# Moving q and k to other byte places in SBUF, in a convolution-attention kernel bound by TensorE

## Chip, cores, metric

One core of a Trainium2 chip. The metric is the device time of one execution in microseconds (us). Each program ran three times or more. Durations of single matmuls are in nanoseconds (ns). In the lines of the profile, PE is TensorE, PEld its weight loads, DVE VectorE, ACT ScalarE and POOL GpSimd; L324 is line 324 of that run's kernel.

## The reference, cut

```python
# x: (4, 64, 64, 256) float32
q = einsum('bwhc,cd->bwhd', x, Wq) + bq          # d = 128
k = einsum('bwhc,cd->bwhd', x, Wk) + bk
v = einsum('bwhc,cd->bwhd', x, Wv) + bv          # d = 256
pq, pk, pv = (t.reshape(B, -1, 4096) for t in (q, k, v))   # a plain reshape, no transpose
attention = softmax(einsum('bcn,bcm->bnm', pq, pk), axis=-1)
out = einsum('bcm,bnm->bcn', pv, attention)
return gamma * out.reshape(B, W, H, C) + x
```

## The kernel before: the parts that matter

float32 products are made from float32r matmuls. q, k, v and the weights x of the softmax are each split: h is the high part, l = x - h the low part, d a difference that carries the rest. A step makes 12 energy matmuls (sa twice and sb once, for four tiles of 128 keys) and 24 for the output: 8 of h with vh, 8 of l with vl (both add into the accumulators a) and 8 of d with vd (into bb). A group is 8 steps for 256 queries; there are 512 steps in all. TensorE's order in the steady loop is always energies, vh, vl, vd, energies.

```python
xpool, xtpool, qkv = pool("xpool", 3), pool("xtpool", 3), pool("qkv", 1)
pool("pad", 1).tile([P, 16], F32, name="pad")
ppool = pool("ppool", 2)                       # x, y, h, l, d
pool("pad2", 1).tile([P, 16], F32, name="pad2")
work, kpool = pool("work", 2), pool("kpool", 3)
...
vh = qkv.tile([P, NM, VC], F32R, tag="vh", name="vh")      # VC = 260: 256 channels, two columns of ones
vl = qkv.tile([P, NM, VC], F32R, tag="vl", name="vl")
vd = qkv.tile([P, NM, C], F32R, tag="vd", name="vd")       # C = 256
...
def energy(b, u, k):
    ...
    for i in range(2):
        for to, f, first, last in ((sa, 0, True, False), (sa, 1, False, True), (sb, 2, True, True)):
            nc.tensor.matmul(to[:, i], kt[:, 2 * k + i, f, :], q[:, f], start=first, stop=last)
...
def attend(b, u):
    ...
    for left, right in ((h, vh), (l, vl), (d, vd)):
        for j in range(NJ):
            out_ = bb[:, j, :] if left is d else acc[j]
            for i in range(4):
                m = 2 * t + i // 2 + NI * (i % 2)
                nc.tensor.matmul(out_, left[:, i, j * P : (j + 1) * P], right[:, m, : out_.shape[1]], ...)
```

In each matmul the first tile (k, h, l, d) is the stationary operand, loaded as weights: 128 columns, 512 bytes of a partition (LDWEIGHTS 128x128 in the profile). The second (q, vh, vl, vd) is the moving one: 256 columns, 1024 bytes, or 258 for vh and vl (MATMUL 128x256 and 128x258), whose two columns of ones give the softmax sums.

**Place** below means a tile's first byte in its partition modulo 256, read from the built program (the prediction gives the same modulo 512). vd is at 32 and d at 96. Rows of vh and vl are 1040 bytes apart, so their places walk in steps of 16. Before, q is at 160 and k at 224.

## Time and profile before

| | |
|---|---|
| time before, median | 2494.4 us (2494.1 to 2496.5 in 3 runs) |
| TensorE busy | 99% of the span |
| energies, 6144 matmuls | 747.4 us from start to start |
| h with vh, 4096 | 494.9 us |
| l with vl, 4096 | 489.8 us |
| d with vd, 4096 | 475.4 us |
| all other matmuls | 276.2 us |

The last five rows are sums of **spacings**. A spacing is the time from a matmul's start to the start of the next one on TensorE. The records of matmuls that follow each other overlap (those of h with vh are 284 ns long in the mean, and start 121 ns apart), so their lengths do not add up to the time; the spacings do. Throughout, a spacing of 114 ns or less is called fast, 117 to 119 slow, and over 140 a gap.

### The profile page before, as it was taken

Reading aid. Unit: us, or ns where it says so; the run is one execution under the profiler, and the core shown is the slowest. Engines: PE = TensorE matmul, PEld = TensorE weight load, DVE = VectorE, ACT = ScalarE, POOL = GpSimd, SP = SyncE. Lnnn points to the kernel's source line nnn. Section 1 sums busy time; section 2 is a strip of 40 time slices with the busy share of each in tenths; the row PEclk is TensorE's granted clock in tenths of the full one; section 3 lists DMA queues with packets and bytes.
Section 4 is the critical chain, followed back from the end, with each engine's and each line's share of the span. In section 5 each row is a group of like instructions: output and inputs, shape, how many; then the busy total and the mean of one; then the engine's idle time right before and its main releaser. Section 6 shows DMA issues by size and latency. Waiting matters only on the chain.

```text
span 2494.6 us, 50085 instructions
## 1 busy us (share of the span) xinstructions
PE 2481.1 (99%) x19982; PEld 2438.4 (98%) x19982; DVE 2106.9 (84%) x2440; ACT 1809.1 (73%) x3138; POOL 425.7 (17%) x780
## 2 busy tenths in 40 slices
PE   9999999999999999999999999999999999999998
PEld 8999999999899999999989999999998999999998
DVE  5888888888698888888869888888886988888887
ACT  5777777777677777777667777777766777777775
POOL 4211111111411111111041111111114111111110
PEclk9999999999999999999999999999999999999999
DMA  7666666664766666666477666666648666666663
GB/s 231 222 195 210 201 201 200 198 202 156 235 220 193 206 199 203 206 188 208 139 244 223 197 193 209 201 208 195 191 145 253 217 201 196 203 203 207 199 193 110
DMA packets 137408, 498.92 MB, mean 200 GB/s; under 512 B 15536, under 2 KB 57264, under 8 KB 137168
## 3 DMA queue, kind: packets, MB, share of 16 engines
q0 software_dynamic: 92320, 453.17, 58.0%
q1 hardware_dynamic: 44304, 42.22, 5.7%
q8 instruction: 160, 2.62, 0.4%
q14 instruction: 80, 0.66, 0.1%
q10 hardware_dynamic: 544, 0.26, 0.0%
HBM read 445.25 MB, written 50.33 MB: 199 GB/s over the span
## 4 chain that ended last, share of the span: by engine, by line
PE 95%; ACT 2%; DVE 1%; issue 1%; DMA 1%; POOL 0%; SPq 0%; ACTq 0%; DVEq 0%; POOLq 0%
PE a L370 38%; PE sa L320 19%; PE bb L370 18%; PE sb L320 10%; PE qk L136 4%; PE v L157 4%; PE ot L416 1%; PE xt L123 1%; ACT h L339 1%; DVE x L334 1%; ACT x L324 0%; ACT y L324 0%; ACT vh L284 0%; DMA kf<-f 0%; DVE vd L287 0%
## 5 line engine op out<-in xcount | busy, mean ns | idle before, releaser
L324 ACT ACTIVATE x<-sa 128x512 f32<-128x512 f32 x1024 | 609.4, 595 | 398.3 <-PE sa L320 330.0
L320 PE MATMUL sa<-q,k 128*128 128x256 f32 x4096 | 757.4, 283 | 1.4 <-ACT x L324 0.9
L334 DVE TENSOR_TENSOR x<-x,y 128x1024 f32<-128x1024 f32 x512 | 625.9, 1222 | 155.6 <-ACT y L324 155.6
L320 PEld LDWEIGHTS sa<-q,k 128*128 128x128 f32 x4096 | 625.7, 189 | 2.8 <-ACT x L324 1.7
L345 DVE TENSOR_TENSOR l<-x,h 128x1024 fp32r<-128x1024 f32 x512 | 624.6, 1220 | 0.0
L348 DVE SCALAR_TENSOR_TENSOR d<-h,x 128x1024 fp32r<-128x1024 f32 x512 | 624.5, 1220 | 0.0
L324 ACT ACTIVATE y<-sb 128x512 f32<-128x512 f32 x1024 | 613.2, 599 | 0.0
L320 PE MATMUL sb<-q,k 128*128 128x256 f32 x2048 | 582.0, 284 | 0.0
L370 PE MATMUL a<-vh,h 128*128 128x258 f32 x4096 | 578.3, 284 | 0.0
L339 ACT ACTIVATE h<-x 128x1024 fp32r<-128x1024 f32 x512 | 543.7, 1062 | 43.1 <-DVE x L334 38.3
L370 PE MATMUL a<-vl,l 128*128 128x258 f32 x4096 | 573.3, 282 | 0.0
L370 PE MATMUL bb<-vd,d 128*128 128x256 f32 x4096 | 557.3, 278 | 0.0
L304 POOL DMA_DIRECT2D k<-kf x512 | 280.5, 548 | 1485.6 <-PE sb L320 1467.0
L370 PEld LDWEIGHTS a<-vh,h 128*128 128x128 f32 x4096 | 526.3, 190 | 0.0
L370 PEld LDWEIGHTS a<-vl,l 128*128 128x128 f32 x4096 | 526.2, 190 | 0.0
L370 PEld LDWEIGHTS bb<-vd,d 128*128 128x128 f32 x4096 | 514.1, 188 | 0.0
L320 PEld LDWEIGHTS sb<-q,k 128*128 128x128 f32 x2048 | 384.5, 188 | 9.4 <-ACT y L324 1.4
L136 PE MATMUL qk<-wqk_sb,xts 128*128 128x256 f32 x512 | 122.8, 383 | 0.0
L400 DVE SCALAR_TENSOR_TENSOR o<-a,o 128x256 f32<-128x256 f32 x126 | 47.6, 420 | 86.9 <-ACT o L380 86.9
L157 PE MATMUL v<-xts,wv_sb 128*128 128x256 f32 x512 | 120.3, 379 | 0.0
L157 PEld LDWEIGHTS v<-xts,wv_sb 128*128 128x128 f32 x512 | 97.3, 190 | 13.2
L408 ACT ACTIVATE o<-o,r 128x256 f32<-128x256 f32 x126 | 57.6, 505 | 72.4 <-DVE r L391 72.4
(54 smaller groups left out, 931.0 us busy)
## 6 DMA issues: line engine op xcount, KB each, us to landing
k<-kf POOLq DMA_DIRECT2D x512, 768.0 KB, 4.8
x<-in_x_dram SPq DMA_DIRECT2D x128, 256.0 KB, 3.6
kf<-f POOLq DMA_DIRECT2D x64, 384.0 KB, 3.8
out_dram<-x POOLq DMA_DIRECT2D x63, 256.0 KB, 2.5
qd<-qks POOLq DMA_DIRECT2D x128, 64.0 KB, 3.0
qr<-qd SPq DMA_DIRECT2D x64, 128.0 KB, 3.0
wv_sb<-in_L_conv_Wv_dram POOLq DMA_DIRECT2D x1, 256.0 KB, 5.7
out_dram<-x SPq DMA_DIRECT2D x1, 256.0 KB, 4.1
```

What stands on the lines that cost most here:

```text
L136: nc.tensor.matmul(qk[:, s, :], self.xt[i][:, k, s, :], wqk_sb[:, k, :], start=(k == 0), stop=(k == KC - 1),)
L157: nc.tensor.matmul(vp[:, eh, :], wv_sb[:, k, eh * P : (eh + 1) * P], self.xt[i][:, k].rearrange("p s a -> p (s a)"), start=(k == 0), stop= ...
L304: nc.gpsimd.dma_start(t.rearrange("p (i s) f d -> p i s (f d)", s=2), kf[b, u % NU])
L320: nc.tensor.matmul(to[:, i], kt[:, 2 * k + i, f, :], q[:, f], start=first, stop=last)
L324: nc.scalar.activation(to[:, 2 * k : 2 * k + 2, :], sp.rearrange("p i j d -> p i (j d)"), AF.Exp, scale=scale,)
L334: nc.vector.tensor_tensor(x, x, y, ALU.mult)
L339: nc.scalar.activation(h, units[b, u], AF.Identity, scale=UPPER)
L345: nc.vector.tensor_tensor(l, x, h.bitcast(F32), ALU.subtract)
L348: nc.vector.scalar_tensor_tensor(d, h.bitcast(F32), 1.0 + E, x, ALU.mult, ALU.subtract)
L370: nc.tensor.matmul(out_, left[:, i, j * P : (j + 1) * P], right[:, m, : out_.shape[1]], start=(t == i == 0 and (left is h or left is d and ...
L400: nc.vector.scalar_tensor_tensor(o[:, j, :], a[:, :C], 1.0 + E, o[:, j, :], ALU.mult, ALU.add)
L408: nc.scalar.activation(o[:, j, :], o[:, j, :], AF.Identity, scale=r[:, j : j + 1])
```

## The change

The intent is to give the energies the same operand places as the vd matmuls that run just before them. Raw q, the loaded q before it is split, drops to one buffer, which makes the room. q's first buffer goes to vd's place, k to d's, and q's second buffer 256 bytes on from the first one's place modulo 512.

```diff
-        pool("pad2", 1).tile([P, 16], F32, name="pad2")
-        work, kpool = pool("work", 2), pool("kpool", 3)
+        pool("pad2", 1).tile([P, 112], F32, name="pad2")
+        work = pool("work", 2)
+        pool("pad3", 1).tile([P, 64], F32, name="pad3")
+        kpool = pool("kpool", 3)
...
-            t = work.tile([P, NJ, P], F32, tag="qr", name=f"qr_{b}_{g}")
+            t = work.tile([P, NJ, P], F32, tag="qr", name=f"qr_{b}_{g}", bufs=1)
...
-            t = work.tile([P, 3, NJ, P], F32R, tag="q", name=f"q_{b}_{g}")
+            t = work.tile([P, 6 * P + 64 * (g % 2)], F32R, tag=f"q{g % 2}", name=f"q_{b}_{g}", bufs=1)
+            t = t[:, 64 * (g % 2) :].rearrange("p (f j d) -> p f j d", f=3, j=NJ)
```

## The prediction

> **What bounds the kernel now.** I read the page's engine shares first, then the chain that ended last, then the groups of instructions, then the engine's waits, then a timeline of TensorE alone.
>
> ```profile
> PE 2481.1 (99%) x19982; PEld 2438.4 (98%) x19982; DVE 2106.9 (84%) x2440; ACT 1809.1 (73%) x3138; POOL 425.7 (17%) x780
> ...
> PE 95%; ACT 2%; DVE 1%; issue 1%; DMA 1%; POOL 0%; SPq 0%; ACTq 0%; DVEq 0%; POOLq 0%
> ```
>
> TensorE and its weight loads are busy all the time and carry 95% of the chain; VectorE has 16% to spare, ScalarE 27%. TensorE's recorded waits for others sum to about 7 us of 2494. So only two things can move the time: the number of matmuls, or the time from one matmul to the next. The instruction order shows the same instructions in the same order on every engine, so the number stays.
>
> ```profile
> L320 PE MATMUL sa<-q,k 128*128 128x256 f32 x4096 | 757.4, 283 | 1.4 <-ACT x L324 0.9 <-DVE q L261 0.5
> L320 PE MATMUL sb<-q,k 128*128 128x256 f32 x2048 | 582.0, 284 | 0.0
> L370 PE MATMUL a<-vh,h 128*128 128x258 f32 x4096 | 578.3, 284 | 0.0
> L370 PE MATMUL a<-vl,l 128*128 128x258 f32 x4096 | 573.3, 282 | 0.0
> L370 PE MATMUL bb<-vd,d 128*128 128x256 f32 x4096 | 557.3, 278 | 0.0
> ```
>
> The second number after the bar is the mean length of one record. The records overlap, so it isn't the spacing, but the differences are real: vd,d is a matmul of the same 256 columns as sa and sb and is 5 to 6 ns shorter. The timeline gives spacing: take the difference of two groups' starts and divide by the count.
>
> ```profile
> 365.14 1.08 PE L370 MATMUL bb<-vd,d 128*128 128x256 f32 x8
> 366.06 0.40 PE L320 MATMUL sa<-q,k 128*128 128x256 f32 x2
> 366.29 0.28 PE L320 MATMUL sb<-q,k 128*128 128x256 f32 x1
> 366.41 0.40 PE L320 MATMUL sa<-q,k 128*128 128x256 f32 x2
> 366.65 0.28 PE L320 MATMUL sb<-q,k 128*128 128x256 f32 x1
> 366.76 0.40 PE L320 MATMUL sa<-q,k 128*128 128x256 f32 x2
> 367.00 0.28 PE L320 MATMUL sb<-q,k 128*128 128x256 f32 x1
> 367.12 0.40 PE L320 MATMUL sa<-q,k 128*128 128x256 f32 x2
> 367.35 0.28 PE L320 MATMUL sb<-q,k 128*128 128x256 f32 x1
> 367.48 1.11 PE L370 MATMUL a<-vh,h 128*128 128x258 f32 x8
> ```
>
> vd,d: 366.06 - 365.14 = 0.92 us for 8, 115 ns each. Energies: 367.48 - 366.06 = 1.42 us for 12, 118 ns each.
>
> **What single starts show.** I joined the start of each of the 19982 matmuls with its operands' addresses in the built program (the order agrees one to one). Spacing here is from one start to the next. Three findings carry the prediction.
>
> - Spacings fall into classes, not a continuum. In vd,d the fourth to seventh matmul of a run of eight is at 113 or 114 ns in 340 to 450 of 512 runs; a run starts at 120.5 ns (mean) and falls by 118.1, 116.0, 114.5 to 114.0. The energies sit at 117 to 119 ns: 4601 of 6144 at 117 to 119, only 562 at 113 or 114; leaving out 227 that are over 140 ns, the mean is 117.6.
> - Both classes hold themselves. After a 113 or 114 in an energy run the next one is that again in 90% of cases; after 117 to 119 again 117 to 119 in 89%. In vd,d the fast class is kept at 96%, but the slow one only at 45%.
> - The energies enter from vd,d, which ends at 113 or 114 in 374 of the 436 cases where energies follow at once. The first energy matmul is then never fast (0 of 374).
>
> At that entry the addresses change. v's d form lies at byte 288 modulo 512 and d at 352; q lies at 416 and k at 480, in all their buffers. The differences are the same (64), the positions are not. In the changed program q's first buffer is at 288, its second at 32, all of k at 352.
>
> [...]equal matmuls differ by 4 to 5 ns, in classes that go with the operands. [...]this trace never has a steady run below 113, so I take 113.5 as the floor.[...]
>
> **The change part by part.**
>
> - *Raw q in one buffer.* It pays for the 256 bytes. The next raw q is loaded some two steps before its halves are made and after the former ones have long been made; a step is 4.3 us and a load lands in 3.0 us (the page's DMA issues). Cost: 0.
> - *The pads and the moved buffers* (q/k scratch, v scratch, the k loads). Same instructions and sizes; VectorE and ScalarE keep their slack. Cost: 0.
> - *q's first buffer with k* (groups 0, 2, 4...: half of the energies, 3072 matmuls). Now nothing changes modulo 512 when TensorE goes from vd,d to energies, so the fast class should carry over and, if lost, be found again within four matmuls as in vd,d. 5917 energies have no long gap, half is 2958; 2958 x (117.6 - 113.5) = 12.1 us if all were fast. vd,d itself has 436 of 512 (85%) fast at its fifth matmul: 12.1 x 0.85 = 10.3. The last energy before vh, now at 122 or 123 in most runs, is in that sum. Against it, one step in eight has transposes ahead of the energies and a stall in them, where the class must be found anew: I take off 1. So -9.5 if the cause is right. I believe in the cause at about 0.75, so -7.
> - *q's second buffer with k* (the other half). Byte 32 against 352: half a period away from vd,d if the period is 512, the same place if it is 256. If the period is 256, another -9. If not, the entry from vd,d shifts the phase as today and the energies settle in some class: the slow one of today (0), or a worse one (121 ns as in the runs of vh, which pass through byte 32 too: 3 ns x 2958 = +9). Weights 0.4, 0.4, 0.2: -3.6 + 0 + 1.8 = about -2.
> - *The rest of the step.* The vh,h run starts with another phase. Its matmuls pass through all places in steps of 16 bytes and wander between 115 and 125; a lasting effect of more than 1 us either way isn't likely.
>
> Sum: -7 - 2 = -9, and slightly more for gains that come together: 2494.4 - 11 = 2483.
>
> **The rivals.**
>
> 1. *Both halves become fast* (period of 256, or the place of k alone matters). For it: at byte 32 in the runs of vh and vl the spacing is 117.9 and 119.1, no worse than at 288 (122.7 and 121.3). Against it: bytes that differ by 256 follow each other in those runs and often alternate high and low (127 then 115), which an equal place would not explain. Time: 2494 - 19 = 2475.
> 2. *The class has nothing to do with addresses*: vd,d is faster[...]. For it: the same differences of 64 give different classes. Against it: energies do hold 113 for whole runs at times, while ScalarE reads just the same, and the classes switch exactly at the entry. Time: 2494, within 2.
> 3. *The second half becomes slower than today* and eats the first half's gain: 2494 to 2497. For it: a byte of 32 against 352 is a difference that no steady run of this kernel has, so there is no evidence that it has a fast class.
> 4. *A faster TensorE runs into ScalarE*: energies need two banks each of sa and sb back. There are 227 energies over 140 ns, with some 25 us above the usual spacing. A step gets shorter by at most 12 x 4 = 48 ns of 4.3 us, about 1%, so these gaps may grow by a few tenths of us in all. This takes 1 or 2 us of the gain at most.
>
> **Range and chances.** Even if every energy went to 113.5 the gain is 5917 x 4.1 = 24 us, 1%. So faster by over 2% (under 2445) has no mechanism. Slower by over 2% would need 8 ns more on each of the 6144 energies, which only spacings at the worst of the whole trace give. The range 2471 to 2495 takes in rival 1 at the low end and rivals 2 and 3 at the high end. Chances: faster 0.01, same 0.98, slower 0.01.
>
> **What would show each step right or wrong.** In the profile after, the energies' mean record should fall from 283 and 284 to about 280 or 281, and vh, vl and vd stay within 1 ns. In the single starts, energies on q's first buffer should be at 113 or 114 in most cases, the first one after vd,d among them; those on the second show which rival holds: fast as well (rival 1), at 117 to 119, or above 120 (rival 3). If the first buffer's energies stay at 117 to 119, the cause I named is wrong (rival 2). If the spacing falls and the time does not, look for longer gaps before sa released by ScalarE (rival 4). The prediction is wrong if the time is under 2471 or over 2495.

## The result

2482.6 us (2482.3 to 2484.3, 4 runs) against 2495.4 (2494.1 to 2496.5, 4 runs). The ratio is 0.995, 95% interval 0.9933 to 0.9968. Ratios here are the mean time of one kernel's runs over that of the other's of the same rounds, so not quite the ratio of the medians quoted.

Engine shares of the kernel after, from its page: the same instructions, TensorE still bound.

```profile
PE 2467.3 (99%) x19982; PEld 2422.2 (98%) x19982; DVE 2103.1 (85%) x2440; ACT 1808.0 (73%) x3138; POOL 425.7 (17%) x780
```

Its matmul groups by form. After the bar: busy us, then the mean ns of one record.

```profile
L324 PE MATMUL sa<-q,k 128*128 128x256 f32 x4096 | 743.1, 280 | 1.1 <-ACT x L328 1.1
L374 PE MATMUL a<-vh,h 128*128 128x258 f32 x4096 | 578.6, 284 | 0.0
L324 PE MATMUL sb<-q,k 128*128 128x256 f32 x2048 | 575.6, 281 | 0.0
L374 PE MATMUL a<-vl,l 128*128 128x258 f32 x4096 | 573.8, 282 | 0.0
L374 PE MATMUL bb<-vd,d 128*128 128x256 f32 x4096 | 558.6, 279 | 0.0
```

sa and sb fall by 3 ns, the other three move by no more than 1. Two steps that follow each other in TensorE's timeline after (first column: start in us), on q's first buffer:

```profile
362.09 1.08 PE L374 MATMUL bb<-vd,d 128*128 128x256 f32 x8
363.00 0.39 PE L324 MATMUL sa<-q,k 128*128 128x256 f32 x2
...
364.36 1.11 PE L374 MATMUL a<-vh,h 128*128 128x258 f32 x8
...
366.27 1.11 PE L374 MATMUL bb<-vd,d 128*128 128x256 f32 x8
367.22 0.40 PE L324 MATMUL sa<-q,k 128*128 128x256 f32 x2
...
368.64 0.64 PE L374 MATMUL a<-vh,h 128*128 128x258 f32 x4
```

In the first, vd takes 363.00 - 362.09 = 0.91 us for 8 (114 ns each) and the 12 energies 364.36 - 363.00 = 1.36 us (113 ns). In the second, vd takes 0.95 us (119) and the energies 1.42 us (118). The energies now run as the vd before them ended. Over the whole trace, of the 436 times that energies follow vd at once, vd ended fast 309 times, and the first energy was then fast 309 times; vd ended slow 127 times, and it was then slow 127 times. Before, it was fast in 0 of 374.

**The account, in sums of spacings.** Energies 747.4 to 733.2 (-14.2), vh +0.2, vl +0.7, vd +1.0, all others -1.3: -13.6 us, and the profiled spans differ by 2494.6 - 2480.9 = 13.7. The two halves of the energies gained alike: 373.6 to 366.6 us on q's first buffer, 373.8 to 366.6 on the second. Leaving out gaps, their spacing went from 117.6 to 114.8 ns, on 5856 matmuls 16.4 us. Some 2.4 us came back in gaps: the last energy before a new group's vh now takes 145 ns in 60 groups (60 x 31 ns = 1.9 us), and the gap in the eighth energy grew from 222 to 230 ns in 64 groups (0.5 us). The first vh matmul of a group, a gap before and after, grew from 171 to 194 ns in 60 groups; that is within the vh row.

What the group's first vh waits for can be read from the trace. It writes the first accumulator a anew, which VectorE reads at the end of the group before, after ScalarE has copied bb. One such place in the timeline after the change (the first line is the last vd matmul of the old group):

```profile
107.70 0.28 PE L374 MATMUL bb<-vd,d 128*128 128x256 f32 x1
...
108.01 0.59 ACT L384 COPY o<-bb 128x512 f32<-128x512 f32 x1 [0.63 <-PE bb L374]
...
108.63 0.76 DVE L404 SCALAR_TENSOR_TENSOR o<-a,o 128x256 f32<-128x256 f32 x2 [1.38 <-ACT o L384]
...
108.95 0.19 PEld L324 LDWEIGHTS sb<-q,k 128*128 128x128 f32 x1
...
109.17 0.30 PEld L374 LDWEIGHTS a<-vh,h 128*128 128x128 f32 x2
```

The first of VectorE's two took 0.43 us, so it ended at 109.06, and the weights of vh load 0.11 us later. In 60 groups, before and after alike, that read ends 1.36 us after the last vd matmul started, and the weight load follows it by 115 or 116 ns. This chain was no shorter for faster energies (1.36 us before and after): TensorE reached it sooner and waited longer, the 145 and 194 ns above.

### The profile page after: what moved, and what is told of

It reads as the page before. It is cut to its first block, busy times and chain, and to the rows that moved or that the text cites.

```text
span 2480.9 us, 50085 instructions
## 1 busy us (share of the span) xinstructions
PE 2467.3 (99%) x19982; PEld 2422.2 (98%) x19982; DVE 2103.1 (85%) x2440; ACT 1808.0 (73%) x3138; POOL 425.7 (17%) x780
## 4 chain that ended last, share of the span: by engine, by line
PE 96%; ACT 2%; DVE 1%; issue 0%; DMA 0%; SPq 0%; ACTq 0%; DVEq 0%
PE a L374 39%; PE bb L374 19%; PE sa L324 18%; PE sb L324 10%; PE qk L136 4%; PE v L157 4%; PE ot L420 1%; PE xt L123 1%; ACT h L343 1%; DVE x L338 1%; ACT x L328 0%; ACT y L328 0%; DMA x<-in_x_dram 0%; DVE vd L289 0%; ACT vh L286 0%
## 5 line engine op out<-in xcount | busy, mean ns | idle before, releaser
L324 PE MATMUL sa<-q,k 128*128 128x256 f32 x4096 | 743.1, 280 | 1.1 <-ACT x L328 1.1
L324 PE MATMUL sb<-q,k 128*128 128x256 f32 x2048 | 575.6, 281 | 0.0
L157 PE MATMUL v<-xts,wv_sb 128*128 128x256 f32 x512 | 120.3, 379 | 0.0
```

Source lines behind the costliest of these rows:

```text
L157: nc.tensor.matmul(vp[:, eh, :], wv_sb[:, k, eh * P : (eh + 1) * P], self.xt[i][:, k].rearrange("p s a -> p (s a)"), start=(k == 0), stop= ...
```

## The experiments

The theory at the start: a spacing class, once reached, holds itself, and the energies inherit vd's class if no operand changes place. Its rivals: the place in itself is fast or slow; only k, or only q, counts; the gain has nothing to do with places. Runs on one chip share their runs of before: e1 to e4 (before: 2496.3 us), e5 to e7 (2494.1), e8 to e10 (2495.9), e11 and e12 (2496.2).

### One operand at a time: e1, e2

```diff
 # e1: k stays at 96, q's second buffer at 160
-            t = work.tile([P, 6 * P + 64 * (g % 2)], ...)
+            t = work.tile([P, 6 * P + 32 * (g % 2)], ...)
-        pool("pad3", 1).tile([P, 64], F32, name="pad3")
+        pool("pad3", 1).tile([P, 96], F32, name="pad3")
 # e2: as e1, with k at 224
+        pool("pad3", 1).tile([P, 128], F32, name="pad3")
```

> The changed kernel, but q's second buffer 128 bytes past the first place instead of 256 (byte 416 modulo 512); k stays at 352. Theory (carry-over: the spacing class that vd,d ends in passes into the energies only if neither operand changes place modulo 256): energies on the first buffer stay as in the changed kernel, 60 to 70% at 113 or 114 ns; those on the second enter with a jump of q by 128, fall back to mostly 117 to 119 (fast share 10 to 20%), and half of the gain goes: 2487 to 2490 us. Rival (only k's place counts): both buffers fast, 2482 to 2484.

> q's first buffer at 288, the second at 416, k back at 480. Carry-over theory: k jumps by 128 at the entry on both buffers, so neither is fast: fast share under 20% on both, 2492 to 2496 us. Rival (only q's place counts): first buffer fast, second not, 2487 to 2490. Rival (a pair with difference 64 is what counts): second buffer (416 with 480) as in the kernel before, first (288 with 480) something else.

Measured: e1 2488.7 us (ratio 0.9971, interval 0.9955 to 0.9988), e2 2488.6 (0.9972, 0.9956 to 0.9989). In e1 the energies on the first buffer were fast in 59% and 115.0 ns in the mean without gaps; on the second in 1% and 117.8. This is one step on the second buffer, in the timeline of e1:

```profile
328.16 1.08 PE L374 MATMUL bb<-vd,d 128*128 128x256 f32 x8
329.07 0.40 PE L324 MATMUL sa<-q,k 128*128 128x256 f32 x2
...
330.49 1.12 PE L374 MATMUL a<-vh,h 128*128 128x258 f32 x8
```

vd is fast here (0.91 us for 8), the energies after it are not (1.42 us for 12). In e2 the first buffer was fast in 62%, the second in 8%. So half the gain went in both, with one buffer of q, and putting k back by 128 bytes cost nothing: the theory's expectation for e2 (2492 to 2496) missed. Of the two operands it was the moving one whose jump of 128 bytes lost the class (1% and 8% fast after it, 59% and 62% without it). The two halves of e1 differ only in q's place, so ScalarE's reads of sa and sb, or anything else in the step, do not explain why one was slow and the other not.

### Nothing but the places: e3, e4

```diff
 # e3: raw q single and q in two tiles as in the change, places as before (q 160, k 224)
-        pool("pad2", 1).tile([P, 112], F32, name="pad2")
+        pool("pad2", 1).tile([P, 16], F32, name="pad2")
-        pool("pad3", 1).tile([P, 64], F32, name="pad3")
-            t = work.tile([P, 6 * P + 64 * (g % 2)], ...)
+            t = work.tile([P, 6 * P], ...)
 # e4: the change, with everything of the loop 128 bytes further
+        pool("pad0", 1).tile([P, 32], F32, name="pad0")
         xpool, xtpool, qkv = pool("xpool", 3), pool("xtpool", 3), pool("qkv", 1)
```

> Placebo: raw q in one buffer and q in two tiles of its own as in the changed kernel, but q back at 416 and k at 480 modulo 512 as before. Carry-over theory: all the gain is gone, 2493 to 2497 us, energies at 117 to 119, fast share about 10%. Rival (the gain comes from the single raw buffer or other moves): 2482 to 2485.

> The changed kernel with all of the loop's tiles moved by 128 bytes together: vd and q at 416, d and k at 480. Carry-over theory: entry places are still equal, so as the changed kernel, 2481 to 2485 us, first energy after vd,d fast whenever vd,d ended fast. Rival (288 with 352 is a fast place in itself, 416 with 480 a slow one, as in the kernel before): energies and vd,d both at 117 to 119: 2496 to 2510 us.

The sa group of e3:

```profile
L323 PE MATMUL sa<-q,k 128*128 128x256 f32 x4096 | 757.2, 283 | 1.1 <-ACT x L327 0.8 <-DVE q L262 0.2
```

And of e4:

```profile
L325 PE MATMUL sa<-q,k 128*128 128x256 f32 x4096 | 742.7, 280 | 1.4 <-ACT x L329 1.2
```

Measured: e3 2495.5 us (0.9997, 0.998 to 1.0013), fast share 9 and 10%, 117.6 ns. e4 2483.0 us (0.9946, 0.993 to 0.9963), fast share 62 and 67%, and of the 312 times that vd ended fast before energies, the first energy was fast 312 times. So the whole gain is the places, and not the place in itself: at 160 with 224, where the kernel before was slow, e4 is as fast as the change.

### Small jumps, and what a class needs: e5, e11

```diff
 # e5: k at 96, q at 48 (16 past vd) and 96 (64 past vd)
-            t = work.tile([P, 6 * P + 64 * (g % 2)], ...)
+            t = work.tile([P, 6 * P + (4, 8)[g % 2]], ...)
-        pool("pad3", 1).tile([P, 64], F32, name="pad3")
+        pool("pad3", 1).tile([P, 108], F32, name="pad3")
 # e11: k at 160, q at 32 and 96
+            t = work.tile([P, 6 * P + 16 * (g % 2)], ...)
+        pool("pad3", 1).tile([P, 128], F32, name="pad3")
```

> The four runs before showed that k's place does not matter and that q's jump against vd modulo 256 does: 0 keeps the class, 128 loses it. Here q's first buffer is 16 bytes past vd's place, the second 64, k at 352. If any jump disturbs: both halves fall back to a fast share of 10 to 20%, 2493 to 2496 us. If only jumps of a sizeable part of 256 disturb: first buffer fast (55 to 70% at 113 or 114), second not, 2487 to 2490. If the period is 64: second fast as well.

> The changed kernel with k 64 bytes further (160 modulo 256), q's first buffer at vd's place 32, the second at 96. Where classes held so far, k minus q was 64 or 192 (64 modulo 128); in the run of small jumps it was 48 and 0, and the fast spacing never followed itself. Theory difference (a class can hold only where k minus q is 64 modulo 128): first buffer (difference 128, 0 modulo 128) has no class that holds, fast followed by fast near 0, mean 118.5 to 120; second (difference 64) has classes that hold, mean 114 to 118. Theory place (q at 32 modulo 128 counts, k never): first buffer as in the changed kernel, 60 to 75% fast, second without a class, 118.5 to 120.

Measured: e5 2499.9 us (1.0025, 1.0008 to 1.0041), slower than before, outside what was expected of the time. Its energies' groups:

```profile
L324 PE MATMUL sa<-q,k 128*128 128x256 f32 x4096 | 765.1, 284 | 0.3
L324 PE MATMUL sb<-q,k 128*128 128x256 f32 x2048 | 585.1, 286 | 0.0
```

Both halves had 118.8 ns without gaps. This was more than a lost inheritance: of 373 fast energies that another energy followed, none was followed by a fast one. The class didn't hold at all. That made the theory as it stood too small, and e11 was built to tell two readings of it apart; the reading "difference" came true. It came to 2497.4 us (1.0006, 0.999 to 1.0023). Its first buffer, at vd's own place but with k at 160, had no fast after fast in 369 cases (mean 118.1); its second, 64 bytes from vd, had 70% fast after fast and 94% slow after slow, and was mostly slow (78%, mean 117.3). All pairs of the energies that ran:

| q, k (modulo 256) | k - q modulo 128 | fast followed by fast | kernel |
|---|---|---|---|
| 160, 224 | 64 | 0.89 and 0.92 | before |
| 32, 96 | 64 | 0.96 and 0.96 | after |
| 160, 96 | 64 | 1.00 (16 cases) | e1 |
| 32, 224 | 64 | 0.97 | e2 |
| 96, 160 | 64 | 0.70 | e11 |
| 48, 96 | 48 | 0.00 | e5 |
| 96, 96 | 0 | 0.00 | e5 |
| 32, 160 | 0 | 0.00 | e11 |

So two conditions showed, for the pairs tried. The fast class held (0.70 to 1.00) only where the stationary place less the moving place was 64 modulo 128; at 48 and 0 it never did (0.00). k does count, but 128 bytes more or less made no difference to it (with q at 32: 0.96 with k at 96, 0.97 at 224), which is why e2 didn't see it. And the class passed from vd into the energies where the moving place stayed the same modulo 256 (fast into fast 309 of 309 times after the change, 312 of 312 in e4). After a jump of 64 (78% slow in e11) or 128 (fast share 1% in e1, 8% in e2; 0 of 374 first energies before) the class entered was mostly the slow one.

The trace of e11 shows one thing more. The last vd matmul before the energies was fast in 0 of 436 cases, 272 of which had the vd before it fast; after the change the two counts are 309 and 309, in e2 343 and 343. Nothing of vd or d had moved: what differs is the place of k, the weights of the matmul that comes next, 128 from vd in place of 64 (192 in e2). So at that point a matmul's spacing went with the difference between its moving place and the stationary place of the next matmul. In a run of energies k has one place, and the two readings are the same.

### The rest of the loop: e6, e7, e8, e10, e9, e12

Once the rule was there, vh and vl (984.7 us of the 2494.6) were next: their places walk, and their matmuls are 258 columns. e6 gives each row of vh and vl one place, 32 and 40, in a common tile of rows of 2304 bytes. The room for it comes from the scratch of q, k and f; e7 makes that second move alone.

```diff
 # e7, on the change: scratch into the rings of l and d
+                now["qk"] = ppool.tile([P, 4, NB], F32, tag="l", ...)[:, :2, :]
+            f = ppool.tile([P, 4, NB], F32R, tag="d", ...)
+            f = f.rearrange("p a n -> p (a n)")[:, : 6 * P].rearrange("p (s j d) -> p s j d", s=2, j=3)
 # e6, on e7
-        vh = qkv.tile([P, NM, VC], F32R, tag="vh", name="vh")
-        vl = qkv.tile([P, NM, VC], F32R, tag="vl", name="vl")
+        vv = qkv.tile([P, NM, 576], F32R, tag="vv", name="vv")
+        vh, vl = vv[:, :, : C + 2], vv[:, :, 258 : 258 + C + 2]
```

> The changed kernel with vh and vl in one tile of rows of 2304 bytes (nine times 256), so that each keeps one place modulo 256 for all rows (32 and 40, vd and q at 32) in place of a walk in steps of 16 bytes; the room comes from q and k scratch and f in the rings of l and d. Carry-over theory, taken further: the whole loop then has no jump over 8 bytes, so vh and vl hold a class as the energies do: 113.5 to 118 in place of 120, 8192 matmuls by 3 to 6 ns = 25 to 50 us less, and vd,d no longer starts its runs at 120: 2425 to 2465 us. Rival (vh and vl are slow because of their 258 columns[...]): they stay at 119 to 121, 2478 to 2486.

> Control for the run of the v rows: the changed kernel with q and k scratch and f in the rings of l and d, vh and vl as they were. Carry-over theory: the places are as in the changed kernel, 2481 to 2486 us. Rival: the shared rings alone move the time, by more than 3 us either way.

Measured: e6 2477.3 us (0.9933, 0.9917 to 0.995), e7 2480.0 (0.9944, 0.9927 to 0.996), both right results and both just under what was expected (the rival's 2478 to 2486 for e6, 2481 to 2486 for e7). e7 against the change is not told apart by these intervals. The hoped-for 25 to 50 us did not come. vh and vl kept their length in e6:

```profile
L375 PE MATMUL a<-vv,h 128*128 128x258 f32 x4096 | 581.9, 285 | 0.0
L375 PE MATMUL a<-vv,l 128*128 128x258 f32 x4096 | 579.7, 284 | 0.0
...
L375 PE MATMUL bb<-vd,d 128*128 128x256 f32 x4096 | 552.7, 278 | 0.0
```

Their spacing was 120.6 and 121.1 ns without gaps, if anything more than after the change (119.7 and 119.8). What e6 gained it gained in the energies and vd: of the 436 runs of energies that follow vd at once, 412 now started fast and none over 116 ns, and the energies were fast in 79 and 82%. The theory, taken further, had failed for vh and vl, so length and place were tried apart, with wrong results on purpose (the sums are replaced by ones, and the measured error is infinite).

```diff
 # e8, on e6 (and e10, on the change): 256 columns
-            out_ = bb[:, j, :] if left is d else acc[j]
+            out_ = bb[:, j, :] if left is d else acc[j][:, :C]
-        nc.vector.tensor_copy(zall[:, b * NG + g, j : j + 1], a[:, C : C + 1])
+        nc.vector.tensor_copy(zall[:, b * NG + g, j : j + 1], ones[:, :1])
 # e9, on e6, right result: 264 columns, vl at place 24 (cut: wider accumulators and a row more, so that the reads stay inside)
-            right[:, m, : out_.shape[1]],
+            (right[:, m] if left is d else vvf[:, m * 576 + (0 if left is h else 318) :])[:, : out_.shape[1]],
 # e12, on e8: vl at vh's place (cut: the columns of ones are no longer written)
-        vh, vl = vv[:, :, : C + 2], vv[:, :, 258 : 258 + C + 2]
+        vh, vl = vv[:, :, :C], vv[:, :, 320 : 320 + C]
```

> Wrong result on purpose (the weights' sums are replaced by ones): the kernel with v rows of 2304 bytes, but vh and vl read 256 columns, without the two columns of ones. Theory A (258 columns are out of step with the other matmuls of 256; the place is not what makes vh and vl slow): vh and vl fall from 121 to 113.5 to 116, the time from 2477 to 2420 to 2440 us. Theory B (vh and vl are slow for their place, 40 bytes against 32[...]): they stay at 119 to 121, 2472 to 2480.

> Wrong result on purpose in the same way: the changed kernel, whose rows of vh and vl walk in steps of 16 bytes, with 256 columns. Theory A with the walk harmless: 113.5 to 116, 2425 to 2440 us. Theory A with a walk that disturbs on its own (as the 16 bytes of q did): vh and vl at 117 to 120, 2465 to 2483.

> Right result: the kernel with v rows of 2304 bytes, vh and vl read 264 columns (six more that nobody uses), and vl lies 8 bytes short of vh's place. If only a length off a multiple of 32 bytes is out of step: vh and vl at 113.5 to 116, 2425 to 2445 us. If any length but 256 is: 120 to 124, 2475 to 2500.

> Wrong result on purpose (no sums, 256 columns): the kernel with v rows of 2304 bytes, vl now at the same place modulo 256 as vh, vd and q (32) instead of 40. In the run before it vh at 32 had the two classes 113 and 118, vl at 40 neither, with 120.3 in the mean and a cycle of three. If the place of 40 made vl slow: all five passes have the two classes, vl at 113 to 118, and the time falls by at least 2.3 ns x 4096 = 10 us to 2435 to 2470; which class dominates decides where in it. If vl is slow [...]for following vh: 119 to 121 still, 2475 to 2482.

Measured: e8 2479.5 us (0.9936, 0.992 to 0.9953), e10 2467.1 (0.9887, 0.987 to 0.9903), e9 2505.2 (1.0037, 1.002 to 1.0054), e12 2440.9 (0.9779, 0.9763 to 0.9795). e10 is within its second expectation and e12 within its first; e9's time lies above both of its own. The groups of e8:

```profile
L375 PE MATMUL a<-vv,l 128*128 128x256 f32 x4096 | 575.8, 283 | 0.0
L375 PE MATMUL bb<-vd,d 128*128 128x256 f32 x4096 | 563.1, 280 | 0.0
L375 PE MATMUL a<-vv,h 128*128 128x256 f32 x4096 | 557.8, 279 | 0.0
```

And of e12:

```profile
L373 PE MATMUL a<-vv,h 128*128 128x256 f32 x4096 | 556.7, 278 | 0.0
L373 PE MATMUL bb<-vd,d 128*128 128x256 f32 x4096 | 554.7, 278 | 0.0
L373 PE MATMUL a<-vv,l 128*128 128x256 f32 x4096 | 554.5, 278 | 0.0
```

Neither expectation for e8 was right as a whole; each was right for one operand. With 256 columns at place 32, vh fell to 115.6 ns and held its class (fast after fast in all of 1738 cases, slow after slow in 98% of 1819). vl at 40 stayed at 120.3 with no fast one, 60% of it at 120 ns or more. In e12, where vl moves to 32, it has 115.0 and all five passes hold both classes. So the length counted (vh at 32: 120.6 with 258, 115.6 with 256), and the place counted (vl: 120.3 at 40, 115.0 at 32; l less vl goes from 56 to 64). A rival to the difference stands untested here: 40 is no multiple of 16 either, while every other place that ran is, but for e9's 24. e8's whole time did not fall below e6's because the vd and energies that follow this vl were slow more often: vd 117.1 ns against 114.5, energies 116.1 against 113.9. With the walk and 256 columns (e10) vh and vl came to 118.2 and 118.0, against 119.7 and 119.8 with 258 (the change):

```profile
L374 PE MATMUL a<-vh,h 128*128 128x256 f32 x4096 | 570.0, 281 | 0.0
L374 PE MATMUL a<-vl,l 128*128 128x256 f32 x4096 | 566.5, 280 | 0.0
```

In e9, 264 columns gave 123.4 and 123.8: padding the length up made these passes longer still (vh 7.8 ns over e8's 115.6 with 256). Its energies were the fastest of all runs (113.7 ns without gaps; vd ended fast in all 436 cases), but that is less than vh and vl lost.

None of e8, e10 and e12 is a kernel to use, as they lack the sums. The fastest right kernel that ran is e6, 2477.3 us; against e7 on the same chip it is only 2.7 us less.

## Why the prediction was right

The predicted time was 2483, the measured 2482.6. Step by step:

- **What bounds, and that nothing else pays:** right. The instruction counts are the same, VectorE's and ScalarE's busy times hardly move (2106.9 to 2103.1 and 1809.1 to 1808.0 us), and the placebo e3 with the single raw buffer took as long as before.
- **The first buffer, -9.5 us if the cause is right, weighed to -7:** the cause held, and the half gained 7.0. The term that was off is the share of fast ones, put at 0.85 as in vd's fifth matmul. The energies were fast in 63%, as vd itself now ended fast in only 309 of 436 (374 before). (And 10.3 less 1 is 9.3, not 9.5.) The step behind it, that a lost class is found again within four matmuls, failed: in the energies after, slow is followed by slow in 93% of cases, so a run that starts slow stays slow, and 127 of 436 do. Slow held itself at the new place as firmly as at the old one (93 and 89%); only the entry changed.
- **The second buffer, -2 us as a mean of three cases:** the first case was the one that came true, a period of 256, with 7.2 us and not 9. What was held against it, that rows of vh 256 bytes apart alternate high and low, does not need a change of place: in e6 vh keeps one place and held no fast class either (0 of 174), and with 256 columns it did (e8, 1738 of 1738).
- **The total:** that it came so close is in part luck. The 7 for the first half was 9.5 times a chance that the cause holds; the cause held, and it was the overrated share of fast ones that brought 9.5 down to 7.0. The second half was put too low (2 for 7.2), and 2 us more had been allowed for gains that come together. So 11 us were forecast, from 2494.4; the means of the runs differ by 12.4 and the profiled spans by 13.7. The 0.4 us between 2483 and 2482.6 is less than the 2 us by which runs of one kernel differ.
- **The rivals:** rival 1 (both halves) is what happened, but at 2482.6 and not at its 2475, since it too had the share of fast ones at 85%. Rival 2 is refuted by e1, rival 3 by the second buffer's 7.2 us. Rival 4 was right in kind and wrong in its place: 2.4 us of the energies' gain came back in gaps, but 1.9 of that just before a new group's vh, not before sa. The wait there is for the accumulators of the group before, which VectorE frees (the weights of vh load 115 or 116 ns after its read), and not for ScalarE to free sa and sb. (The waits of TensorE that the profile records sum to 5.2 us before, not to about 7; nothing rests on it.)
- **The entry:** the prediction took a change of either operand for the cause. e1 and e2 show that it was the moving one; k mattered only through the difference (no fast after fast at 48 and 0, e5 and e11).

Open: why a class held at 64 modulo 128, and why a jump led to the slow one; no run here shows the cause beneath the places. Nor was k moved by steps finer than 64, and e5's jump of 16 came with a difference of 48, so a jump of 16 alone was not tried.

## What to carry to other kernels

Where TensorE is busy all the time, read starts, not lengths: here the spacing of equal matmuls showed two classes, 113 to 114 and 117 to 119 ns, some 4% apart, that went with where the operands lie. The addresses alone moved the energies from 117.6 to 114.8 ns (e3 against after). For these matmuls of 256 float32r columns with 128-column weights, what was fast was a moving place that stayed the same modulo 256 from one pass to the next (309 of 309 fast entries) and a stationary one, that of the next matmul too, 64 from it modulo 128 (fast after fast 0.70 to 1.00, against 0.00 at 48 and 0). Finer steps of k and other kernels were not tried, so check on the chip: one placement cost time (e5, 2499.9 us against 2494.1). Row strides that walk, and two columns too many, cost as much as a bad place here: 1040-byte rows some 3 ns per matmul (vl, 118.0 in e10 against 115.0 in e12), two columns 5 (vh, 120.6 in e6 against 115.6 in e8), and both together some 5 (vl, 119.8 after the change against 115.0 in e12).
